# Graph attention and a transformer layer on one core: preparation steps in two halves, rows kept on chip, keys by transfer, tail loads and norms during attention

## The chip, the cores and the metric

The kernel runs on one core of a Trainium2 chip. The core has TensorE (matrix products, PE in the profile, with its weight loads as PEld), VectorE (DVE), ScalarE (ACT), GpSimd (POOL) and SyncE (SP), which here issues every transfer. The metric is the device time of one execution in microseconds (us), as a median of several runs.

## The reference

Two graph attention layers, then one transformer layer, over 4096 nodes with 256 features; `adj` is a 4096 x 4096 matrix of zeros and ones. Everything is float32.

```python
def gat_layer(x, adj, W, a):                  # 8 heads of 32
    Wh = einsum('nd,hdo->hno', x, W)
    src, dst = Wh . a[:, :32], Wh . a[:, 32:]
    e = leaky_relu(src[:, :, None] + dst[:, None, :], 0.2)
    alpha = softmax(where(adj > 0, e, -9e15))
    return heads_side_by_side(alpha @ Wh)

h = elu(gat_layer(x, adj, W1, a1)) + x
x = elu(gat_layer(h, adj, W2, a2)) + h

q, k, v = layer_norm(x, g1, be1) @ w_qkv      # 8 heads of 32
scores = where(adj != 0, q k^T / sqrt(32), -inf)
x = x + (softmax(scores) @ v) @ w_proj + b_proj
out = x + gelu(layer_norm(x, g2, be2) @ w1 + b1) @ w2 + b2
```

## The kernel before

The nodes are 32 tiles of 128. There are three stages, each in a function of its own or part of one.

**Graph attention** (`graph_attention`). The work of a layer is cut into groups: 4 blocks of 8 row tiles, times 4 pairs of heads, times 8 groups `g` of 4 column tiles, so 128 groups a layer and 256 in all, indexed by `i`. The exponential of a leaky ReLU factors on each side of its kink, so a group needs no exponential of its own: it needs a comparison of two terms per pair of nodes (`step` in `compare`, ScalarE's Sign at line 1100 or VectorE's comparison at line 1102), the adjacency laid over it as bits (line 1115, one VectorE operation a group) and then matmuls with the prepared values `vst` (line 1401, TensorE). Comparisons for group `i + 2` are made during group `i`.

Before a layer can run, `preparation(l, q, ...)` must make the values of eight groups of four tiles, `q` from 0 to 7. Its steps are: `features` (transposes at line 981 into a PSUM bank, ScalarE's copy at 984), `values` for each of four tiles (matmuls at 994 into a bank, then ScalarE's copy and three exponentials at 1001 to 1008, VectorE's maximum and product at 1009 and 1020), `split` (a float16 part and its remainder, 1032 to 1035, the last on GpSimd) and `term_rows` (one transpose, a copy and four small stores). For layer 0, `q` of 2 to 7 are prepared in groups 0 to 5; in the same groups the adjacency is read, clipped by VectorE (867) and turned by TensorE and ScalarE (`mask_turn`, 890 and 892). For layer 1, `q` of 0 to 5 are prepared in the last six groups of layer 0, and 6 and 7 in groups 131 and 132. Steps and turns take a bank from a ring of two (`turn_bank`).

Within a group all such extra steps are put into a list `side` with a place between 0 and 1, sorted by it, and emitted among the matmuls: after each of the group's eight row tiles come those whose place has been reached (lines 1401 to 1412). TensorE, ScalarE and VectorE run in exactly that order; SP and GpSimd are ordered by a scheduler outside the first lines. `pair_end` finishes a pair of heads in seven later steps; `step_out` adds the result to the layer's input and stores it, and `rows_ahead` loads four tiles of the stored rows for the preparation of the next layer.

**Query, key, value** (first part of `unshifted_transformer`). For each of 8 blocks of 512 nodes: norm, transposes, the projections (line 1677 for queries and keys, each stored to memory in a float16 part and its remainder; line 1696 for values). Keys are then loaded back by `stack` into `k_st`, which holds four stacked parts of 32 partitions for each head: two by transfer, the other two copied by VectorE at line 1710. Only SP's order is fixed here.

**Attention.** A unit is a block of queries, a half `c` of the heads (four, a quad) and one key tile, 512 units in all. A unit is scores (line 1734), the exponential (1741, ScalarE), the mask (1743, VectorE, two operations a unit), then the weighted sum of values (`u_av`, 1752) and the sum of weights (`u_dn`, also 1752); GpSimd adds the weights of two units first (`u_both`, 1825). At a quad's end the sums are stored, the denominators go to memory and back as `u_dens`, VectorE inverts them (1794) and the inverses are stored. TensorE, ScalarE and VectorE run in written order.

**The tail.** For each block of 512: load rows, attention sums and inverses (`rows_of`), apply bias and inverses, project (1888), add, norm (1448 to 1477), transpose (1490), first linear (1924) with GELU (1931), second linear (1940), store. The next block's projection stands ahead of the first linear. The scheduler orders all engines here.

Of the kernel before, what the change touches and what calls it, by code (L numbers as in the profile page):

```python
# [22 lines left out]
P = 128  # L23
# [728 lines left out]
def graph_attention(  # L752
# [127 lines left out]
    def mask_turn(nb, c, i):  # L880
# [8 lines left out]
        for m in range(G):  # L889
            nc.tensor.transpose(pt[:, m, :], v[:, m * P : (m + 1) * P], ident_h)  # L890
        to = built[nb, c][:, i // 2].bitcast(U16)
        nc.scalar.activation(to[:, :, i % 2 * P : (i % 2 + 1) * P], pt.bitcast(U16), AF.Copy)
        if i % 2 == 1:
            w = STARTS[0][nb] // PER + i // 2
            nc.sync.dma_start(
                mask_d[w][c], built[nb, c][:, i // 2].rearrange("p g n -> p (g n)").bitcast(U8)
            )

# [66 lines left out]
    def rows_ahead(l, q):  # L965
        if q < NG:
            coming_rows[l, q] = rows_p.tile([P, G, D], F32, name="g_rows")
            rows[l].load(coming_rows[l, q], G * q)

    def preparation(l, q, bank, first=False):  # L970
# [4 lines left out]
        def features(c):  # L975
# [3 lines left out]
            pt = bank()  # L979
# [4 lines left out]
            nc.scalar.copy(L.ft[q][:, c, :], pt)  # L984
            if c == DC - 1:
                del coming_rows[l, q]
                if (l > 0 or q > 1) and (l == 0 or q + 1 != NG - 2):
                    rows_ahead(l, q + 1)

        def values(t):  # L990
            at = G * q + t
            pv = bank()
            for c in range(DC):
# [7 lines left out]
            nc.scalar.copy(  # L1001
                L.terms[:, :, at, :], pv[:, D : D + 2 * H].rearrange("p (k h) -> p k h", k=2)
            )

            big = some.tile([P, 2, H], F32, name="g_big", bufs=4)
            for i, scale in enumerate((-1.0, -LRELU)):
                nc.scalar.activation(big[:, i, :], pv[:, D + H : D + 2 * H], AF.Exp, scale=scale)
            nc.scalar.activation(L.r[:, at, :], pv[:, D : D + H], AF.Exp, scale=LRELU - 1.0)
            nc.vector.tensor_reduce(
# [27 lines left out]
        def term_rows():  # L1037

            pr = bank()[: G * H, :P]
            nc.tensor.transpose(  # L1040
                pr, L.terms[:, 0, G * q : G * (q + 1)].rearrange("p t h -> p (t h)"), ident_f
            )
            sr = some.tile([G * H, P], F32, name="g_sr", bufs=1)
            nc.scalar.copy(sr, pr)
# [4 lines left out]
        steps = [lambda c=c: features(c) for c in range(DC)]  # L1049
        for t in range(G):  # L1050
            steps.append(lambda t=t: values(t))
            if t > 0:
                steps.append(lambda t=t: split(t - 1))
        return steps + [term_rows, lambda: split(G - 1)]
# [67 lines left out]
    def pair_end(l, nb, p, ev):  # L1122
# [6 lines left out]
        held = {}  # L1129
        wide = [P, n, 2, V1]  # L1130
# [51 lines left out]

        def step_out():
# [9 lines left out]
            [step_exp], [step_below, step_above], [step_out],  # L1193
# [55 lines left out]
    def begin():  # L1249
# [21 lines left out]
        first, second = (preparation(0, q, spare_bank, True) for q in range(2))  # L1271
        for step in first[:DC] + second[:DC]:
            step()
        for step in weights_steps(0):
            step()
        del first[:DC], second[:DC]
        value = [[steps[k] for k in (0, 1, 3, 5)] for steps in (first, second)]
        part = [[steps[k] for k in (2, 4, 6, 8)] for steps in (first, second)]
        row = [steps[7] for steps in (first, second)]
        for step in value[0][:2]:  # L1280
            step()
        for k in range(2):
            clip(k)
            value[0][2 + k]()
        row[0]()
        for k in range(4):
            value[1][k]()
            part[0][k]()
            if k < 2:
                clip(2 + k)  # L1290
            if k > 1:
                part[1][k - 2]()
        row[1]()
        s_of[0, 0, 0] = s_fetch(0, 0, 0)
        rows_ahead(0, 2)
        for k in range(4):
            turn(k)
            if k < 2:
                part[1][2 + k]()
# [16 lines left out]
    for i, (l, nb, p, g) in enumerate(groups):  # L1316
# [12 lines left out]
        if i + 1 in prepared and prepared[i + 1][0] > 0:  # L1329
            if prepared[i + 1][1] in (0, NG - 2):  # L1330
                rows_ahead(*prepared[i + 1])
        if made:
            steps = preparation(*made, lambda: turn_bank([P, 512], F32))
            if made[1] == NG - 1:
                steps.append(lambda: check_values(made[0]))
            beside(steps, 0.0, 0.9)
        if i + 2 < len(groups):
            steps = compare(i + 2)
            beside(steps[:-1], 0.25 if made else 0.0, 0.95)
# [8 lines left out]
        beside([lambda u=u: mask_turn(*u) for u in turns.get(i, ())], 0.0, 0.9)  # L1348
# [21 lines left out]
        for n in range(tiles):  # L1370
            w, at = n // PER, slice(n % PER * P, (n % PER + 1) * P)
            for m in range(G):
# [25 lines left out]
                for at_, (k, to, left, right) in enumerate(todo):  # L1398
# [3 lines left out]
                    opened.add(k)  # L1402
            if g == NG - 1:
# [7 lines left out]
            while side and (n == tiles - 1 or side[0][0] * tiles < n + 1):  # L1411
# [156 lines left out]
def unshifted_transformer(  # L1568
# [47 lines left out]
    dens = wts.tile([P, NQ, QI], F32, name="u_dens")  # L1616


    with ExitStack() as scope:
        vals = scope.enter_context(tc.tile_pool(name="u_vals", bufs=1))  # L1620
        k_st = vals.tile([P, DC * HC, N], F16, name="u_k")
        v_sb = vals.tile([P, NT, D], F32, name="u_v")
        blocks = scope.enter_context(tc.tile_pool(name="u_blocks", bufs=2))
        masks = scope.enter_context(tc.tile_pool(name="u_masks", bufs=5))
        block_tiles = {}

        def stack(to, i, order, cols):

            for a, kind in enumerate(order):
                if kind is None:  # L1630
                    continue
                first = half_d[i, kind, 0, 0:1, cols]
                nc.sync.dma_start(
                    to[a * O : (a + 1) * O],
                    spread(first, [[N, O], [O * N, DC * HC], [1, NB]]),
                )

        def load_queries(nb):
            q_st = blocks.tile([P, DC * HC, NB], F16, name="u_q")
            stack(q_st, 0, (0, 1, 0, 1), slice(nb * NB, (nb + 1) * NB))  # L1640
# [10 lines left out]
        with ExitStack() as qkv:  # L1651
# [8 lines left out]
            for nb in range(NNB):  # L1660
# [8 lines left out]
                if 2 < nb + 2 < NNB:  # L1669
                    ahead.moments(nb + 2)  # L1670
                    ahead.normed(nb + 2)
# [33 lines left out]
                for b in (nb - 1,) if nb + 1 < NNB else (nb - 1, nb):  # L1705
                    if b >= 0:
                        at = slice(b * NB, (b + 1) * NB)
                        stack(k_st[:, :, at], 1, (0, None, 1, None), at)
                        for o in (0, 2 * O):
                            nc.vector.tensor_copy(k_st[o + O : o + 2 * O, :, at], k_st[o : o + O, :, at])  # L1710
# [14 lines left out]
        def weights(nb, c, mt, u):  # L1725
# [4 lines left out]
            for j in range(2):  # L1730
                h = c * HC + 2 * u + j
                for r in range(HC):
# [3 lines left out]
                        k_st[:, h, at : at + O],  # L1736
# [64 lines left out]

# [261 lines left out]
```

## Time and profile before

| | us |
|---|---|
| three runs | 3217.39, 3220.55, 3221.06 |
| median | 3220.55 |
| profiled execution, device time | 3218.54 |
| its span in the profile | 3216.7 |
| PE busy in the span | 3091.4 (96%) |
| DVE busy | 2809.8 (87%) |
| ACT busy | 2667.1 (83%) |
| POOL busy | 1175.5 (37%) |

How to read it: a time in the page is one execution's. Graph attention lasts to about 1644 us, the query, key and value part to 1733, attention to 2926, the tail to the end. A busy share of 96% is an average over these; what is missing is in a few places, which a table of busy time by window shows. The chain of waits follows what ended last back to what released it, and so tells which wait counts.

### The profile page before, as it was taken

The numbers are of one execution on the slowest core, as the hardware profiler recorded it, in microseconds if no ns is written. First come the engines' busy times: TensorE is split into PE (matmuls) and PEld (weight loads), VectorE is DVE, ScalarE is ACT, GpSimd is POOL, SyncE is SP. The second block draws the span as 40 slices with busy tenths as digits, with TensorE's granted clock in tenths as the row PEclk, the third lists the DMA queues.
The fourth block names the chain that finished last, engine by engine and source line by source line (L and its number), as shares of the span: only waits on it lengthen the run. The fifth ranks groups of instructions, "written<-read, shape, count | busy, mean of one in ns | idle before, by whom it ended". The sixth has DMA issues, their size and how long they took to land.

```text
span 3216.7 us, 139103 instructions
## 1 busy us (share of the span) xinstructions
PE 3091.4 (96%) x64076; PEld 2713.3 (84%) x64076; DVE 2809.8 (87%) x3198; ACT 2667.1 (83%) x3175; POOL 1175.5 (37%) x536
## 2 busy tenths in 40 slices
PE   5899999999889999999998999999999999997999
PEld 4799999999779999999975888888888888885766
DVE  7899999989879999999986999999999999995221
ACT  6899999999779999999965888888888888884231
POOL 2300000000220000000002988899989889884110
PEclk8999999999999999999999999999999999998999
DMA  8666554420310312121145010101011010004110
GB/s 257 202 196 206 163 191 147 145 84 26 97 52 25 94 55 89 33 64 53 45 122 138 14 40 21 34 26 28 28 27 50 8 47 14 21 7 120 59 46 28
DMA packets 210305, 249.29 MB, mean 77 GB/s; under 512 B 87792, under 2 KB 131056, under 8 KB 209712
## 3 DMA queue, kind: packets, MB, share of 16 engines
q1 hardware_dynamic: 209712, 240.31, 24.5%
q8 instruction: 503, 8.24, 1.0%
q14 instruction: 90, 0.74, 0.1%
HBM read 197.80 MB, written 42.47 MB: 75 GB/s over the span
## 4 chain that ended last, share of the span: by engine, by line
PE 47%; DVE 3%; ACT 2%; DMA 1%; issue 0%; SPq 0%; DVEq 0%; ACTq 0%
PE u_ps L1734 15%; PE u_av L1752 14%; PE u_dn L1752 8%; PE misc L1940 3%; PE misc L1924 3%; PE misc L1677 2%; ACT t L1100 1%; DVE t L1115 1%; DVE t L1102 1%; PE misc L1696 1%; PE misc L1888 1%; PE misc L1490 0%; DVE u_e L1743 0%; DMA u_wide<-inv_d 0%; DVE u_k L1710 0%
## 5 line engine op out<-in xcount | busy, mean ns | idle before, releaser
L1401 PE MATMUL bank<-vst,t 128*128 128x132 f16 x16384 | 1449.8, 219 | 25.8 <-DVE t L1115 25.3
L1825 POOL TENSOR_TENSOR u_both<-u_e 128x1024 f32<-128x1024 f32 x448 | 1052.5, 2393 | 914.7 <-DMA u_k<-half_d 787.0
L1401 PE MATMUL bank<-vst,mask 128*128 128x66 f16 (+1 forms) x10296 | 1344.7, 206 | 0.0
L1100 ACT ACTIVATE t<-s_b,g_terms 128x1024 int8<-128x1024 f32 x1231 | 1318.5, 1155 | 27.4 <-PE bank L1401 21.6
L1401 PEld LDWEIGHTS <-t 128*128 128x128 fp8e4 x16384 | 1184.0, 97 | 40.2 <-DVE t L1115 29.7
L1743 DVE SCALAR_TENSOR_TENSOR u_e<-u_mask,u_ps 128x1024 f32<-128x1024 uint8 x1024 | 1165.9, 1214 | 9.2 <-ACT u_ps L1741 5.0
L1741 ACT ACTIVATE u_ps<-u_ps 128x1024 f32<-128x1024 f32 x1024 | 1030.0, 1009 | 141.8 <-PE u_ps L1734 45.6
L1401 PEld LDWEIGHTS <-mask 128*128 128x128 fp8e4 x10296 | 902.2, 98 | 0.0
L1115 DVE SCALAR_TENSOR_TENSOR t<-mask,t 128x2048 int32<-128x2048 int32 x256 | 591.0, 2309 | 73.6 <-ACT t L1100 63.1
L1734 PE MATMUL u_ps<-u_q,u_k 128*32 128x512 f16 x8192 | 636.6, 383 | 10.4 <-DVE u_e L1743 7.8
L1752 PE MATMUL u_av<-u_e,u_v 128*32 128x128 f32 x16384 | 601.2, 273 | 0.0
L1752 PEld LDWEIGHTS u_av<-u_e,u_v 128*32 128x32 f32 x16384 | 487.6, 110 | 130.1 <-issue 1.7
L1102 DVE TENSOR_SCALAR t<-s_b,g_terms 128x1024 fp8e4<-128x1024 f32 x817 | 583.8, 747 | 2.6 <-DMA s_b<-s_d 2.6
L1035 POOL TENSOR_TENSOR vst<-g_prod,vst 128x528 f16<-128x528 f32 x36 | 44.0, 1236 | 778.0 <-DVE vst L1034 757.7
L1752 PE MATMUL u_dn<-u_both,u_ones 128*32 128x128 f32 x7168 | 279.6, 273 | 0.0
L1734 PEld LDWEIGHTS <-u_k 128*32 128x32 f16 x8192 | 227.4, 95 | 57.9 <-issue 16.4
L1752 PEld LDWEIGHTS u_dn<-u_both,u_ones 128*32 128x32 f32 x7168 | 212.2, 110 | 41.4 <-issue 0.4
L1931 ACT ACTIVATE u_hid<-misc,n_b 128x512 f32<-128x512 f32 x64 | 42.4, 687 | 152.5 <-PE misc L1924 152.4
L1947 DVE TENSOR_TENSOR u_xres<-u_xres,misc 128x256 f32<-128x256 f32 x32 | 13.5, 421 | 141.9 <-PE misc L1940 141.9
L1940 PE MATMUL misc<-u_w,u_hid 128*128 128x256 f32 x512 | 111.8, 379 | 0.0
L1924 PE MATMUL misc<-ln_cols,u_w 128*128 128x512 f32 x256 | 111.2, 592 | 0.0
L1940 PEld LDWEIGHTS misc<-u_w,u_hid 128*128 128x128 f32 x512 | 96.7, 190 | 13.3 <-issue 0.5
(145 smaller groups left out, 1865.3 us busy)
## 6 DMA issues: line engine op xcount, KB each, us to landing
g_adj<-in_adj_dram SPq DMA_DIRECT2D x123, 512.0 KB
s_b<-s_d SPq DMA_DIRECT2D x64, 512.0 KB
mask<-mask SPq DMA_DIRECT2D x128, 256.0 KB
u_mask<-mask SPq DMA_DIRECT2D x32, 512.0 KB
mask<-stage SPq DMA_DIRECT2D x48, 256.0 KB
rows<-e_x SPq DMA_DIRECT2D x32, 256.0 KB
half_d<-u_halves SPq DMA_DIRECT2D x32, 256.0 KB
u_q<-half_d SPq DMA_DIRECT2D x32, 256.0 KB
```

Of the source, the lines that this page charges most:

```text
L1100: nc.scalar.activation(to.bitcast(I8), s, AF.Sign, bias=negd, scale=-1.0)
L1102: nc.vector.tensor_scalar(to, s, negd, -1.0, op0=ALU.is_ge, op1=ALU.mult, saturate=False)
L1115: nc.vector.scalar_tensor_tensor(both, m32.unsqueeze(1).to_broadcast(list(both.shape)), SIGNS, both, op0=ALU.bitwise_or, op1=ALU.bitwise_and,)
L1401: nc.tensor.matmul(to, left, right, start=k not in opened, stop=last)
L1677: nc.tensor.matmul(pq, wq_sb[k][:, i * D + c * P : i * D + (c + 1) * P], hn[:, k, :], start=(k == 0), stop=(k == DC - 1),)
L1734: nc.tensor.matmul(ps[r * O : (r + 1) * O, j, :], k_st[:, h, at : at + O], q_st[:, h, :], start=True, stop=True,)
L1741: nc.scalar.activation(ps, ps, AF.Exp, scale=SCALE)
L1743: nc.vector.scalar_tensor_tensor(e, mask, 0.0, ps, op0=ALU.not_equal, op1=ALU.mult)
L1752: nc.tensor.matmul(to[j * O : (j + 1) * O, at], lefts[j], es[j // 2][:, j % 2, at], start=first and part == 0, stop=last and part == PARTS ...
L1825: nc.gpsimd.tensor_tensor(both, es_of[i - 1][u], es_of[i][u], op=ALU.add)
L1924: nc.tensor.matmul(ph, w1_sb[:, k, f * P : (f + 1) * P], hn[:, k, :], start=(k == 0), stop=(k == DC - 1),)
L1940: nc.tensor.matmul(po[:, :D], hid[:, f, at : at + P], w2_sb[:, f, :], start=(f == 0), stop=(f == FC - 1),)
```

## The change

It has five parts.

1. *Steps in two halves.* In `preparation`, each use of a bank is split into an `_out` half (TensorE) and an `_in` half (ScalarE and VectorE); `mask_turn` likewise. A group places the two halves and `split` by slots, turns and values taking turns in layer 0. Side steps are emitted after each of a group's 32 sets of matmuls and no longer after each of its 8 row tiles. In `values`, the exponentials come ahead of the copy.

```diff
+    def features_out(c):
+        pt = held["f", c] = bank()
+        for t in range(G):
+            nc.tensor.transpose(...)
+    def features_in(c):
+        nc.scalar.copy(L.ft[q][:, c, :], held.pop(("f", c)))
...
+            uses = list(features)
+            delay = 0.3 if turning else 0.6
+            for t in range(G):
+                if turning:
+                    u = turning.pop(0)
+                    uses.append((lambda u=u: turn_out(*u), lambda u=u: turn_in(*u)))
+                uses.append(values[t])
+            uses.append(term_rows)
+            slot = 0.9 / len(uses)
+            for k, use in enumerate(uses):
+                side.append(((k + 0.5) * slot, use[0]))
+                side.append(((k + 0.5 + delay) * slot, use[1]))
+                if use in values:
+                    side.append(((k + 2.0 + delay) * slot, splits[values.index(use)]))
...
-            beside(steps[:-1], 0.25 if made else 0.0, 0.95)
+            beside(steps[:-1], 0.3 if made else 0.0, 0.95)
...
+                while side and side[0][0] * tiles * G < n * G + m + 1 and not (
+                    n == tiles - 1 and m == G - 1
+                ):
+                    side.pop(0)[1]()
...
-            while side and (n == tiles - 1 or side[0][0] * tiles < n + 1):
+            while side and n == tiles - 1:
```

2. *Rows kept.* The last pair of layer 0's last block writes its result straight into the row tiles that `q` of 6 and 7 of layer 1 read; their other columns are loaded at the layer's start.

```diff
+        keeps = l + 1 < NL and first + n == NT and p + 1 == H // 2
...
+        def step_out_and_keep():
+            x, ex = held["x"], held["ex"]
+            for k in range(n // G):
+                to = coming_rows[l + 1, first // G + k][:, :, cols]
+                nc.vector.tensor_tensor(to..., x[:, k * G : (k + 1) * G], ex[...], op=ALU.add)
+                nc.sync.dma_start(rows[l + 1].blocks[nb][...], to)
...
+        if l > 0 and (nb, p, g) == (0, 0, 0):
+            for q in (NG - 2, NG - 1):
+                rows_ahead(l, q, D - 2 * O)
```

3. *Keys.* `k_st` is two tiles, one for each half of the heads. For the last three blocks all four parts come by transfer. A one-element exponential after the last norm brings ScalarE's table in early.

```diff
+                        for c in range(DC):
+                            late = b >= NNB - 3
+                            kinds = (0, 0, 1, 1) if late else (0, None, 1, None)
+                            stack(k_st[c][:, :, at], 1, kinds, at, c, HC)
+                            for o in () if late else (0, 2 * O):
+                                nc.vector.tensor_copy(
+                                    k_st[c][o + O : o + 2 * O, :, at], k_st[c][o : o + O, :, at]
+                                )
...
+                        nc.scalar.activation(rooted, ahead.held[nb + 2][:, 0, 1:2], AF.Exp)
```

4. *Loads and first operations during attention.* At the fifth unit of the last quad, `load_early` loads the tail's weights and biases and the rows, sums and inverses of blocks 0 and 1, into the key tile of the first half of the heads, and into a query and a mask buffer. GpSimd applies bias and inverses. A one-element root follows the last exponential.

```diff
+                    if u == 0 and units[i] == (NNB - 1, DC - 1, 4):
+                        load_early()
...
+            for k, unit in enumerate(((NNB - 1, DC - 1, NT // 2 - 1), units[-1])):
+                if i < len(units) and units[i] == unit:
+                    res, att, inv = early[k]
+                    nc.gpsimd.tensor_tensor(
+                        res, res, early["bp"].to_broadcast([P, TB, D]), op=ALU.add
+                    )
+                    nc.gpsimd.tensor_tensor(att, att, inv, op=ALU.mult)
+            if i == len(units) - 1:
+                nc.scalar.activation(rooted, norms.eps, AF.Sqrt)
...
+            slab = slab_p.tile([P, 32 * D], F32, name="u_k0")
+            two = blocks.tile([P, 2, TB * D], F32, name="u_q")
+            for nb in range(2):
+                load_rows(nb, *early[nb])
```

5. *Order of the tail.* Blocks 0 and 1 are projected first; block `nb + 2` is projected after the first linear of block `nb`. TensorE runs in written order. The check of the denominators comes at block 2.

```diff
+        scope.enter_context(tc.manual_schedule(engines={mybir.EngineType.PE}))
+        ready = [projected(*early[nb][:2]) for nb in range(2)]
+        coming = rows_of(2)
+        hn = turned(ready[0][1])
...
         for nb in range(NNB):
+            res, res_n = ready.pop(0)
...
-                res_next, res_n = projected(*rows_of(nb + 1))
...
+            if nb + 2 < NNB:
+                ready.append(projected(*coming))
+                if nb + 3 < NNB:
+                    coming = rows_of(nb + 3)
             if more:
-                hn = turned(res_n)
+                hn = turned(ready[0][1])
```

## The prediction

> **What bounds the kernel now.** I read the 40 slices first, then busy time by window, then the chain of waits and the VectorE timeline inside the windows that were not full.
>
> The slices (PE = TensorE, DVE = VectorE; each digit is a tenth of a slice of 80.4 us):
>
> ```profile
> PE   5899999999889999999998999999999999997999
> DVE  7899999989879999999986999999999999995221
> PEclk8999999999999999999999999999999999998999
> ```
>
> TensorE is full nearly everywhere. There are four dents: the first two or three slices, slices 11 and 12, slice 22, and slice 37. Busy time in windows cut at those dents (start:end, length, then busy us of PE, weight load, DVE, ACT, POOL, then granted clock, DMA share, GB/s):
>
> ```profile
> 91.80:107.90 16.10, 12.39 (x149) 10.48 (x149) 11.81 (x23) 11.08 (x31) 9.13 (x6) 1.00 0.67 216
> 834.10:847.40 13.30, 10.80 (x133) 9.30 (x131) 12.04 (x22) 8.08 (x26) 5.12 (x5) 1.00 0.21 60
> 922.20:941.30 19.10, 15.33 (x157) 13.55 (x157) 9.63 (x19) 9.29 (x28) 4.26 (x4) 0.82 0.24 69
> 1733.00:1760.00 27.00, 16.87 (x272) 10.88 (x276) 25.41 (x20) 15.03 (x17) 13.90 (x5) 0.75 0.53 118
> 1790.00:2926.50 1136.50, 1134.90 (x32664) 916.24 (x32652) 1123.63 (x1002) 1004.36 (x1018) 1013.47 (x433) 1.00 0.10 26
> 2926.50:2961.60 35.10, 14.54 (x40) 11.46 (x41) 12.04 (x32) 2.42 (x4) 6.97 (x3) 0.61 0.68 200
> 2961.60:3209.00 247.40, 247.40 (x921) 169.76 (x919) 49.77 (x148) 70.50 (x98) 30.55 (x13) 1.00 0.16 50
> ```
>
> Attention (fifth line) and the feed-forward (last) have no idle TensorE to win. What can be won lies in the others: groups that also prepare values (first three), the start of attention, and the gap before the feed-forward. The timeline of line 1115 (one mask operation per group) gives their lengths: the six groups that prepare for layer 0 start 14.05, 15.40, 14.45, 16.11, 15.39 and 14.87 us apart (90.3), the first six for layer 1 take 83.4 us, and its last two 19.0 and 15.1. A group without preparation takes about 5.2 to 6.3.
>
> The start of attention, chain of waits (start, length, what):
>
> ```profile
> 1737.61 3.48 DVE u_e L1743 x3
> 1741.12 1.22 DVE u_k L1710
> 1742.37 2.35 DVE u_e L1743 x2
> 1744.75 3.20 DVE u_k L1710
> ```
>
> VectorE's key copies (L1710) stand in the queue between the score masks (L1743) that TensorE waits for. The gap before the feed-forward, same view:
>
> ```profile
> 2926.83 3.10 DMA den_d<-u_den
> 2930.01 4.04 DMA u_dens<-den_d
> 2943.75 9.86 DMA u_wide<-inv_d
> 2953.72 1.24 DVE u_att L1884
> 2955.01 6.78 PE misc L1888 x16
> 2961.79 13.73 PE misc L1924 x32
> ```
>
> Here the end waits for transfers: the last denominators go out and back, then loads for block 1 stand behind two weight loads of 1 MB.
>
> **What the skill says.** "TensorE: Matmul & The Clock Gate", "What's actually happening": the array starts throttled, and only sustained work releases it. The trace agrees: granted clock 0.61 in the gap, 0.75 at the start of attention, 1.00 in full windows. So a gap costs more than its idle time. "DMA: Bandwidth & Descriptors", "Queues, rings and completion order": each engine takes descriptors in ring order, and all of SP's transfers share one row. The trace agrees: a 128 KB load took 9.86 us behind the weights. This is my warning for loads moved into attention. "ScalarE: Activation LUTs", "What ACT_TABLE_LOAD costs", gives about 1283 ns plus a drain; the trace has 1283 ns.
>
> **The change, part by part** (against the profiled execution: 3218.54 us, span 3216.7).
>
> *Loads and norms ahead (the end).* Weights, biases and rows, attention and inverses of blocks 0 and 1 are loaded in the last quad (a block's four heads), and POOL applies bias and inverses there. After the last attention matmul (about 2925.2) TensorE can project at once, with full clock. Two projections (L1888 x16, 3.45 us each for later blocks in the chain) end at 2932.1. Block 0's chain on VectorE: the last add comes about 3.6 us after the start; behind it stand 2 adds and 2 statistics of block 1's (0.42 each) and an aggregate or two (0.18), then the inverse (0.17) and four norms (1.38): about 7.6 us. Transposes of the last tile and ScalarE's ln_cols (0.78 each, two, partly overlapped) make some 9. The first L1924 then starts at 2934.3, where it now starts at 2961.6: 27.3 us gained. Both cases have the same work behind that point, 247.4 us of full TensorE; moving a projection from before the first linear to behind it changes no total. The last denominators still travel, but only block 7's projection needs them. Bounds: 24 (VectorE's order delays the norm) to 28. The Sqrt table is loaded after the last exponential, beside matmuls: nothing.
>
> *What that costs in attention.* SP can issue the early loads once the last read of the first key half is done, about 2846 (3 us before VectorE's first mask of the last quad). Some 2 MB go before the quad's denominators, w1 (1 MB) just before, w2 just behind them. Now u_dens is issued at 2858.9 and VectorE's reciprocal stands at 2864.6, with the masks (1.146 us each: 73.35 us a quad over 64) queued behind it. At 200 to 300 GB/s (windows above, slices) w1 delays the denominators by 1 to 2 us and w2 the reload by 3 to 5, so the reciprocal is late by about 1, 0 to 4. If the whole 4 MB stood ahead it would be 20 us; that end is a rival. POOL gets four operations of 2.35 us; TensorE reads u_both some 4.5 us after it is ready (u_both ends 2856.4, read 2861.0). Two fall into the quad's idle POOL time of 3.7 us, but one of them waits for its load, and one follows the first pair: about 5.1 us late against 4.5, cost about 1, 0 to 4. Together I take 2, range 0 to 8.
>
> *Keys by transfer.* The six copies of the last three blocks on VectorE between 1735.03 and 1754.9 (2.47 for two, then 1.22, 3.20, 1.22, 2.02) go; the earlier blocks' are only cut in halves. Thirteen masks are done at 1761.6 now; from 1737.61 at 1.146 each they would be at 1752.5: 9.1 gained, plus about 0.4 since the Exp table is loaded earlier (the load stands at 1735.08, first exponential 1736.37), less some slow clock. I take 9.3, bounds 6 (slow clock lasts) and 11. In exchange SP issues 24 transfers instead of 6, about 0.5 us each: 9 us more, and 1.5 MB more. Those keys are first used 20 units of 2.29 us into attention, 46 us later, so that hides; SP's following query load is wanted two quads later.
>
> *Split bank steps.* Nothing is removed. TensorE's half and the reading half get separate places, at a step of 1 in 32 of a group instead of 1 in 8, and ScalarE may do comparisons between them. A preparing group has 11 to 12.4 us of TensorE and 10.4 to 13.1 of VectorE against 13.3 to 16.1, so the most that could go is about 2.5 a group. But two banks serve all steps: a value step holds one for TensorE (1.0 us), three exponentials (0.2 each), a reduction and a product (0.42, 0.68), some 2.7 plus what stands ahead on ScalarE and VectorE, four times a group, and in layer 0 turns and values alternate, so that values always get the same bank. I take 0.85 a group for these twelve: 10. Bounds: minus 3 to 28, since no row shows the new order.
>
> *Rows kept.* Layer 1's last two groups (19.0 and 15.1) no longer wait for the row's way to memory and back (longest wait there 3.4 us, then a clock of 0.82). TensorE's 15.33 busy at 0.82 are 12.5 at full clock. I take 13 for each: 8.5, bounds 3.4 and 11. VectorE pays two adds of half size (0.42) for one of 0.69.
>
> Sum: 27.3 + 9.3 + 10 + 8.5 - 2 = 53.1; 3218.5 - 53.1 = 3165.4. The median shown is 2.0 above the profiled execution, so 3167.4.
>
> **Rivals** (medians).
> - The split gains nothing, the banks bind as now: only 3.4 of the rows is left. 27.3 + 9.3 + 3.4 - 2 = 38: 3182.5. For it: VectorE is 12.04 of 13.30 busy already. Against: in the window from 91.80 no engine is busy for more than 12.4 of 16.1 us.
> - The split brings preparing groups near the busiest engine, 12.6 in layer 0 and 11.6 in layer 1: 14.7 + 13.8, rows 10. With the rest 73.1: 3147.5.
> - The early loads delay the denominators of the last quad by the whole 4 MB, VectorE's reciprocal holds the masks for 20 us: 3187. For it: ring order, as above. Against: most of it is issued 11 us before.
> - Slower: value steps sharing one bank stretch each of the 14 preparing groups, since the read half now comes later behind comparisons. It decides from 3.2 us a group (the 38 of the first rival and 6.4, over 14). At 4 us a group: 3220.5 - 38 + 56 = 3238.5. Against: the reading half is moved by a third to six tenths of a slot only, under 0.5 us of matmuls.
>
> **How the numbers follow.** Forecast 0.62, no gain from the split 0.18, near the floor 0.10, loads in the way 0.05, slower 0.05. The range 3149 to 3187 holds the forecast with its bounds, the first rival and half of the second. A difference under 0.2% (6.4 us) can't be told from none here; all cases but the last are faster by more, so faster 0.94, same 0.01, slower 0.05.
>
> **What would show it.** Right: the first L1924 (now another line) within 10 us of the last attention matmul, at a clock near 1; no key copy among the first masks, and the first 13 of these in about 15 us; preparing groups of 14 and 13 us; no group of 19. Wrong: an idle VectorE ahead of u_inv in the last quad; TensorE waiting for u_both there; a VectorE or ScalarE queue that keeps the turn banks, with preparing groups as long as now.

## The result and the profile after

The changed kernel takes 3169.9 us (median of 4 runs, 3168.24 to 3172.45), the kernel before 3218.97 in its runs beside it: ratio 0.985, 95% interval 0.983 to 0.987. The forecast was 3167.4. The profiled execution has a span of 3168.0 us, 48.7 less than before. The slices after:

```profile
PE   6999999999989999999999999999999999999999
DVE  7899999989899999999985999999999999998221
PEclk8999999999999999999999999999999999999999
```

The dents of TensorE at slices 11, 22 and 37 are gone, one at slice 12 and the ones at the start remain. Busy time in windows cut at the mask operation (one a group, now line 1129): the six preparing groups of layer 0, the first six of layer 1, and layer 1's last two with the groups around them.

```profile
48.40:132.40 84.00, 70.78 (x862) 60.75 (x860) 73.92 (x132) 64.80 (x172) 34.86 (x23) 1.00 0.74 228
815.00:890.40 75.40, 66.30 (x812) 57.96 (x810) 66.87 (x118) 54.16 (x162) 36.40 (x22) 1.00 0.40 118
890.40:954.60 64.20, 56.60 (x966) 53.59 (x963) 60.71 (x84) 52.44 (x91) 17.77 (x10) 1.00 0.12 35
```

Before, the same stretches took 90.3, 83.4 and 69.0 us:

```profile
47.93:138.20 90.27, 74.16 (x903) 62.88 (x901) 73.60 (x137) 64.24 (x177) 35.43 (x24) 0.99 0.66 211
820.62:903.98 83.36, 72.33 (x859) 62.67 (x858) 66.98 (x118) 55.01 (x161) 28.52 (x24) 0.96 0.33 103
```

VectorE and ScalarE have the same work in them within 0.9 us, and VectorE now is busy for 88 and 89% of the first two. TensorE's records show 41 and 47 matmuls fewer in them. A stretch is cut at VectorE's mask operations, and part of TensorE's work now falls into the group behind it: the group behind the first stretch takes 8.0 us instead of 6.7, the one behind the second 9.7 instead of 8.1. So of the 6.3 and 8.0 us by which the first two are shorter, some is only moved: with the next two groups counted in, the first gains 5.7; with the next three, the second gains 6.0. The start of attention, VectorE's timeline (start, length, what, and idle time before it):

```profile
1720.09 15.93 DVE L1818 SCALAR_TENSOR_TENSOR u_e<-u_mask,u_ps 128x1024 f32<-128x1024 uint8 x14 [2.71 <-ACT u_ps L1816]
1737.60 8.01 DVE L1818 SCALAR_TENSOR_TENSOR u_e<-u_mask,u_ps 128x1024 f32<-128x1024 uint8 x7 [1.58 <-ACT u_ps L1816]
```

Fourteen masks stand back to back with no copy between them; then comes a pause of 1.58 us. Before, pauses of 0.83 and 0.16 us stood about there. The last quad, idle time of TensorE, and then the chain of waits at its end:

```profile
2832.56 0.86 PE L1827 MATMUL u_av<-u_e,u_v 128*32 128x128 f32 x24 [1.32 <-issue]
2837.40 0.64 PE L1827 MATMUL u_av<-u_e,u_v 128*32 128x128 f32 x16 [0.29 <-issue]
2843.37 0.30 PE L1827 MATMUL u_dn<-u_both,u_ones 128*32 128x128 f32 x2 [0.77 <-POOL u_both L1936]
```

```profile
2902.95 0.48 PE u_dn L1827 x16
...
2903.49 0.59 ACT u_den L1860
2904.09 0.04 issue
2904.13 7.17 PE misc L1985 x32
2911.30 0.50 PE misc L1545 x4
...
2911.89 0.79 ACT ln_cols L1548
2912.68 0.04 issue
2912.72 14.00 PE misc L2024 x32
```

No transfer is left in this chain. From the last attention matmul to the first linear it takes 9.3 us, before 36.4. From there to the end it is 255.3 us (before 255.1).

### The profile page after: what moved, and what is told of

Same layout as the page of the kernel before. It is cut to its first block, busy times and chain, and to the rows that moved or that the text cites. A ratio compares the mean times of both kernels' runs of the same rounds, so it can differ in the third digit from the quotient of the medians.

```text
span 3168.0 us, 139144 instructions
## 1 busy us (share of the span) xinstructions
PE 3073.6 (97%) x64076; PEld 2705.3 (85%) x64076; DVE 2809.0 (89%) x3201; ACT 2668.9 (84%) x3177; POOL 1197.6 (38%) x538
## 3 DMA queue, kind: packets, MB, share of 16 engines
q8 instruction: 503, 8.24, 1.1%
## 5 line engine op out<-in xcount | busy, mean ns | idle before, releaser
L1114 ACT ACTIVATE t<-s_b,g_terms 128x1024 int8<-128x1024 f32 x1231 | 1318.9, 1157 | 31.4 <-PE bank L1452 24.4
L1818 DVE SCALAR_TENSOR_TENSOR u_e<-u_mask,u_ps 128x1024 f32<-128x1024 uint8 x1024 | 1166.1, 1215 | 15.1 <-ACT u_ps L1816 10.2
L1049 POOL TENSOR_TENSOR vst<-g_prod,vst 128x528 f16<-128x528 f32 x36 | 59.5, 1669 | 748.2 <-DVE vst L1048 735.6
L2044 PE MATMUL misc<-u_k,u_hid 128*128 128x256 f32 x512 | 111.8, 379 | 0.0
L2024 PE MATMUL misc<-ln_cols,u_k 128*128 128x512 f32 x256 | 111.3, 593 | 0.5 <-ACT ln_cols L1548 0.5
L2044 PEld LDWEIGHTS misc<-u_k,u_hid 128*128 128x128 f32 x512 | 96.7, 190 | 13.3 <-issue 0.5
L2024 PEld LDWEIGHTS misc<-ln_cols,u_k 128*128 128x128 f32 x256 | 48.6, 190 | 58.5 <-issue 56.9
```

The costliest lines, as they stand in the source:

```text
L1049: nc.gpsimd.tensor_tensor(halves[:, :, 1, :], part, halves[:, :, 0, :], op=ALU.subtract)
L1114: nc.scalar.activation(to.bitcast(I8), s, AF.Sign, bias=negd, scale=-1.0)
L1818: nc.vector.scalar_tensor_tensor(e, mask, 0.0, ps, op0=ALU.not_equal, op1=ALU.mult)
L2024: nc.tensor.matmul(ph, w1_sb[:, k, f * P : (f + 1) * P], hn[:, k, :], start=(k == 0), stop=(k == DC - 1),)
L2044: nc.tensor.matmul(po[:, :D], hid[:, f, at : at + P], w2_sb[:, f, :], start=(f == 0), stop=(f == FC - 1),)
```

## The experiments

Every kernel below was timed with runs of the kernel before beside it (their median was 3217.4 for the first four, 3219.3 for the next four, 3217.6 for the last). Since effects of 2 to 5 us are near what the total can tell, I read them from stages of the trace. The table holds, in us: the median; layer 0's six preparing groups; layer 1's first six; the stretch of its last two; from the first attention mask to the first denominators' reciprocal; from the fourteenth reciprocal to the last attention matmul; from there to the first linear.

| kernel | median | L0 | L1 | last two | start | last quads | to linear |
|---|---|---|---|---|---|---|---|
| before | 3219.0 | 90.3 | 83.4 | 69.0 | 97.8 | 134.0 | 36.4 |
| changed | 3169.9 | 83.9 | 75.4 | 64.2 | 90.1 | 137.3 | 9.3 |
| steps_whole | 3181.7 | 90.6 | 83.5 | 62.8 | 88.6 | 138.3 | 9.3 |
| halves_together | 3181.5 | 80.8 | 84.7 | 69.7 | 90.2 | 137.3 | 9.3 |
| halves_coarse | 3175.1 | 84.7 | 75.4 | 67.7 | 91.4 | 137.3 | 9.3 |
| rows_back | 3177.5 | 83.9 | 75.4 | 69.6 | 90.5 | 138.3 | 9.3 |
| keys_copied | 3182.2 | 83.9 | 75.4 | 65.4 | 99.4 | 138.3 | 9.3 |
| layer0_together | 3167.0 | 82.0 | 75.4 | 65.4 | 90.0 | 137.8 | 9.3 |
| steps_whole_fine | 3177.8 | 90.3 | 81.7 | 62.4 | 90.4 | 138.3 | 9.3 |
| paced | 3180.6 | 83.9 | 75.4 | 65.4 | 90.1 | 143.3 | 9.3 |
| slab_after | 3178.5 | 84.8 | 75.4 | 65.4 | 90.1 | 134.0 | 20.9 |
| burst_and_order | 3182.4 | 83.9 | 75.4 | 66.8 | 89.5 | 138.6 | 23.3 |
| turns_after | 3175.3 | 89.5 | 75.4 | 65.4 | 90.0 | 136.9 | 9.3 |
| act_paced | 3166.1 | 82.0 | 75.4 | 65.4 | 88.7 | 137.5 | 9.3 |

A stage before attention that a kernel does not touch repeats within 1 us, the last two groups' stretch within 2.6. In attention the same code differs by some us: see the last section.

**Preparation put back whole.**

```diff
-                side.append(((k + 0.5) * slot, use[0]))
-                side.append(((k + 0.5 + delay) * slot, use[1]))
...
+            def whole(use):
+                return lambda: (use[0](), use[1]())
+            beside(steps, 0.0, 0.9)
...
+            while side and (n == tiles - 1 or side[0][0] * tiles < n + 1):
```

> The preparation steps of graph attention are put back as before: both halves of a bank use at one place, the old order of steps, places only after each row tile, statistics from 0.25. Everything else as changed. Theory A (these places and halves made the preparing groups shorter): the six preparing groups of layer 0 go back from 84.0 to about 90 us and the first six of layer 1 from 75.4 to about 83, so the whole is 12 to 16 us slower (about 3182 to 3186). Theory B (the twelve groups got shorter through something else, such as rows already in SBUF or the order of the exponentials): these sums stay within 3 us of 84.0 and 75.4, the whole under 5 us slower.

90.6 and 83.5, 14.8 us more together, and 11.8 in the median: theory A holds. The part of the new steps is real and larger than I forecast. The third stretch is 1.4 us shorter than in the changed kernel: the group behind layer 1's six and the one behind its last two are 1.7 and 2.1 us shorter, while group 6 (the first of the last two) takes 12.8 us instead of 10.4. With the groups behind counted in, the new steps are worth 12.6 us.

**Halves apart or together, fine places or coarse.** In halves_together the reading half has no delay; in halves_coarse the emission between a tile's matmuls is taken out.

```diff
-                side.append(((k + 0.5 + delay) * slot, use[1]))
+                side.append(((k + 0.5) * slot, use[1]))
```

> As changed, but the reading half of each bank use comes at the same place as TensorE's half; slots, order and the fine places stay. Theory A1 (it is the distance between the halves that helps): layer 0 and layer 1 groups lose most of the 14.3 us, the whole is 8 to 14 us slower. Theory A2 (it is the fine places and the turns between values that help): the two sums rise by less than 4 us together.

> As changed, halves apart, but steps are only given out after a row tile (8 places a group), no longer between its matmuls (32 places). Theory A1 (the distance between halves helps): a slot of 0.9/9 of a group is about a tile, so the halves still lie a tile apart and the sums stay within 4 us. Theory A2 (fine places help): the whole is 8 to 14 us slower, sums near 90 and 83.

Neither theory holds for both layers. With the halves together layer 1 loses 9.3 us in its six groups and 5.5 in its last two, as A1 says, but layer 0 gains 3.1: the delay harms it. Coarse places cost 0.7 in layer 0 and nothing in layer 1's six; 3.4 in the last two. So in layer 1 the gain needs the distance. The waits in layer 1's six groups (us in total, times, longest), with halves together:

```profile
DVE g_prod L1034 <- POOL vst L1049: 19.8, 14, 2.8
PE turn L1054 <- DVE g_prod L1034: 14.6, 6, 2.5
ACT g_sr L1060 <- PE turn L1054: 14.4, 6, 2.6
```

and in the changed kernel:

```profile
DVE g_prod L1034 <- POOL vst L1049: 6.2, 6, 1.4
PE turn L1054 <- DVE g_prod L1034: 4.6, 5, 1.3
ACT g_sr L1060 <- PE turn L1054: 0.7, 1, 0.7
```

The transpose of the term row (L1054) needs a bank that VectorE's product (L1034) still holds, and the product itself waits for GpSimd's remainder (L1049). With both halves at one place ScalarE's reading half (g_sr) sits in its queue meanwhile, 2.4 us a group, with all comparisons behind it. Put later, it waits 0.7 us in all.

The old order of steps did not have this wait. In steps_whole, same six groups:

```profile
ACT g_big L1018 <- PE turn L1005: 17.8, 17, 3.1
ACT g_sr L1060 <- PE turn L1054: 0.7, 2, 0.4
```

There ScalarE waits for the values' matmuls instead, 17.8 us against 10.6 in the changed kernel. So the distance keeps the new order from bringing a wait of its own; what in the new order removed the old wait of layer 1 was not taken apart.

**Layer 0.** Three kernels take it apart. steps_whole_fine gives the old list out at fine places; layer0_together keeps the halves together in layer 0 only; turns_after is that kernel with the mask turns at places of their own. With the turns out of the list, its values stand 0.13 of a group apart and no longer 0.16, and two of its four turns still fall between values.

```diff
+                side.append(((k + 0.5 + (delay if made[0] else 0.0)) * slot, use[1]))
...
-                if turning:
+                if False:
                     u = turning.pop(0)
```

> As changed, but with the old list of steps (whole steps, turns after the values, statistics from 0.25) given out at the new fine places between a tile's matmuls. Theory A5 (layer 0 gains from turns between values and parts two slots later, not from fine places): layer 0's six groups stay near 90, layer 1's near 83, the whole 11 to 15 us slower. Theory A2 (fine places): layer 0 falls to 84 or below.

> As changed, but in layer 0, where mask turns alternate with values, the reading half of a bank use comes at the same place as TensorE's half; layer 1 keeps the distance. Theory A3 (between two banks that alternate turn and value, a later read only keeps the bank longer; in layer 1 it fills TensorE's wait): layer 0's six groups fall from 84.0 to about 81, layer 1's six stay at 75.4 within 0.5, the whole 2 to 4 us faster than the changed kernel. Theory A4 (the two stages depend on each other through the statistics ahead): layer 1 changes by more than 2 us.

> As the kernel with layer 0's halves together, but the mask turns of layer 0 are spread over the group at places of their own instead of one ahead of each value step. Theory A5 (a turn ahead of each value gives every value step the same bank with a turn's time to come free, which is what layer 0 gained): its six groups go back from 82.0 to 88 or more, the whole 6 to 9 us slower than that kernel. Rival A6 (new slots, parts two slots later and the statistics' later start are what gained): under 84.

The fine places alone give layer 0 nothing (90.3) and layer 1 1.8 us. Layer 0 falls to 82.0 with halves together while layer 1 stays at 75.4 (A3), and goes back to 89.5 when the turns have places of their own (A5's number). So its gain is the list in which a turn comes one place ahead of each value; how much of that is the turn and how much the wider spacing of the values was not taken apart. What TensorE and ScalarE wait for in layer 0's six groups, in turns_after:

```profile
ACT g_big L1018 <- PE turn L1005: 20.7, 20, 3.2
PE turn L1005 <- DVE ev_broad L1040: 6.3, 5, 2.0
```

in layer0_together:

```profile
ACT g_big L1018 <- PE turn L1005: 7.4, 17, 0.9
PE turn L1005 <- ACT mask L898: 5.2, 18, 0.6
```

and in the changed kernel:

```profile
ACT g_big L1018 <- PE turn L1005: 16.1, 22, 1.3
PE turn L1005 <- ACT t L1114: 7.0, 12, 1.5
PE turn L1005 <- DVE ev_broad L1040: 3.3, 4, 1.1
```

The largest difference is ScalarE's: the value's reading half (g_big) stands in its queue until TensorE has made the value (L1005), 20.7 us in turns_after and 7.4 in layer0_together. TensorE in turn waits for a bank. In turns_after that is up to 2.0 us for another value's product (ev_broad; L1034 is the operation that reads the bank, L1040 the one behind it). In layer0_together all 18 waits end 0.05 us after the copy of the turn just ahead (L898), 14 of them before the product of the value before has ended: a value takes over the turn's bank, and waits 0.6 at most.

With the halves apart it is the other way. In the changed kernel 15 of the 24 values begin 0.15 us after the product (L1034) of the value before has ended, most of them while the turn between is still being copied: values keep to one bank and wait for each other, mostly 0.5 to 0.7 us. The profile puts 11 of these 15 waits down to a comparison (t, L1114) that ended at about the same time; but in the other four the distance to the product is the same, so I take it for the product. Values that share one bank were the mechanism of my slower rival. It exists, at 2 to 3 us for six groups instead of 24.

**Rows through memory again.**

```diff
-        keeps = l + 1 < NL and first + n == NT and p + 1 == H // 2
+        keeps = False
...
-        if l > 0 and (nb, p, g) == (0, 0, 0):
-            for q in (NG - 2, NG - 1):
-                rows_ahead(l, q, D - 2 * O)
```

> As changed, but layer 1's last two row groups again go through memory and back in whole (VectorE adds in one operation and nothing is kept). Theory R1 (the row's wait is what was gained, and part was given back by the groups after): group 6 goes back from 10.4 to about 19 us, the stretch from the first of the last two to the last group's end from 64.2 to about 68 to 69, the whole 4 to 5 us slower. Theory R2 (my prediction's 8.5): 8 to 9 us slower. Theory R3: the split steps would have hidden the wait anyway, under 2 us slower.

The median is 7.6 us slower, but only 5.4 of it are in the stage: group 6 takes 15.8 us, not 10.4, and not the 19.0 of before, so the split steps had already taken 3.2 of its wait. TensorE waits 2.2 us there for the row. R1's size holds for the stretch (4.2 to 5.4, since its other groups repeat only within 1.2), R1's 19 us does not. The groups behind the six and behind the last two take 9.7 and 7.2 us as in the changed kernel, where steps_whole has 8.1 and 5.0 as before; so what these two lost belongs to the split, not to the rows. The rest of the median is not the rows': in the profile, attention, whose code is the same, is 3.4 us longer, with 8.2 us of stalls marked issue against 3.9.

**Keys copied again.**

```diff
-                            late = b >= NNB - 3
+                            late = False
```

> As changed, but the keys of the last three blocks are again copied by VectorE instead of coming by transfer. Theory K1 (my prediction's 9.3, of which the changed kernel showed 7.4 because the added 1.5 MB leave TensorE without instructions for 1.7 us): VectorE's copies stand between the first masks again, the stretch from the first mask to the first reciprocal goes from 90.1 back to about 97.8, the stall of TensorE marked issue among the first masks (1.67 us at 1735.60) is gone or under 0.3 us, the whole 7 to 8 us slower. Theory K2 (the stall has nothing to do with transfers): the stall stays at 1.5 us or more and the stretch is about 99.5.

Of the twelve half-size copies four stand just ahead of the first mask and eight between the first masks, where before four whole ones stood. The first of these eight (VectorE's timeline):

```profile
1720.55 2.35 DVE L1818 SCALAR_TENSOR_TENSOR u_e<-u_mask,u_ps 128x1024 f32<-128x1024 uint8 x2
1722.94 0.68 DVE L1783 COPY u_k<-u_k 32x2048 f16<-32x2048 f16 x1
1723.65 1.22 DVE L1818 SCALAR_TENSOR_TENSOR u_e<-u_mask,u_ps 128x1024 f32<-128x1024 uint8 x1
1724.90 3.43 DVE L1783 COPY u_k<-u_k 32x2048 f16<-32x2048 f16 x2
```

Both theories are half right. No stall among the first masks is marked issue any more, as K1 says, but TensorE waits for masks there in the meantime (3.25 us at the longest), and a stall could hide in these waits. The stretch is 99.4, as K2 says, 9.4 more than in the changed kernel: the copies in halves cost more than the whole ones did (97.8).

**Early loads spaced by SP's written order.** Attention runs SP in written order; block 1 and the pieces of w1 and w2 are written one in every second unit.

```diff
+        ordered.add(mybir.EngineType.SP)
...
+                    if u == 0 and paced and units[i][2] > 7 and i % 2 == 0:
+                        paced.pop(0)()
```

> As changed, but SP's work in attention follows the written order, and of the early loads only the projection's weight, the biases and block 0 come at once; block 1 and eight pieces of w1 and w2 (256 KB each) follow one in every second unit. Theory F (a burst of transfers delays TensorE's own instruction loads): the stalls marked issue in the last quad (1.6 us) fall under 0.4 us, the last 14 to 16 units' masks no longer wait, the stretch from the fourteenth reciprocal to the last attention matmul falls from 137.3 to about 134, the whole 2 to 4 us faster. Theory P (POOL's four added operations cost it): the stretch stays above 136.

A miss, and a useful one: it is 11 us slower. The loads wait for nothing, so SP issued them all between 2838 and 2860, where their places in the program are spread over 22 units (some 50 us): an order is not a clock. And now the 2 MB written ahead of the reload of the denominators (u_dens) stand ahead of it: SP issues it 7.5 us after the store it follows, in all other quads but the last 2.1 to 2.4. VectorE's timeline:

```profile
2850.90 0.25 DVE L1869 RECIPROCAL u_inv<-u_dens 128x16 f32<-128x16 f32 x1 [6.13 <-DMA u_dens<-den_d]
```

The masks behind the reciprocal wait 6.1 us. This is my rival of loads that hold the denominators, met here and not in the changed kernel. The Trainium skill, "DMA: Bandwidth & Descriptors", "Queues, rings and completion order", has descriptors taken in ring order on each DMA engine. Here some 5 of the 6.1 us lie in the later issue by SP; what the rings add, no run here separates.

That is half of the loss. The other 5 us lie before the last quads. SP's written order now puts each block's query load and a mask load next to each other, and TensorE stalls behind them in six blocks, 0.7 to 1.8 us each and 7.6 in all (0.6 in the changed kernel), the first of them here:

```profile
1892.57 0.52 PE L1827 MATMUL u_av<-u_e,u_v 128*32 128x128 f32 x10 [1.07 <-issue]
```

**The slab over the other half of the keys.**

```diff
-            pool.tile([P, HC, N], F16, name=f"u_k{c}") for c, pool in enumerate((slab_p, vals))
+            pool.tile([P, HC, N], F16, name=f"u_k{c}") for c, pool in enumerate((vals, slab_p))
...
-            slab = slab_p.tile([P, 32 * D], F32, name="u_k0")
+            slab = slab_p.tile([P, 32 * D], F32, name="u_k1")
```

> As changed, but the slab of early loads lies over the second half of the keys, which attention reads to its end: projection weight, biases, block 0's rows, attention and inverses, w1 and w2 can only start with the last scores; block 1's loads stay early. Theory T (my prediction: the end was gained by loads that no longer stand behind attention, at a small cost in the last quad): from the last attention matmul to the first linear it takes 20 to 28 us instead of 9.3, and the last quad is free of w1, w2 and POOL's bias operations, so the stretch from the fourteenth reciprocal to the last attention matmul falls from 137.3 to about 134; the whole 8 to 15 us slower. Rival T2 (the end was gained by the order of projections): the gap stays under 14 us.

Both numbers of theory T came: 20.9 and 134.0. TensorE sits idle 10 us at the end:

```profile
2910.65 4.64 PE L1985 MATMUL misc<-u_k 128*128 128x256 f32 x10 [10.03 <-POOL u_k L1953]
```

So the early loads of the slab, with GpSimd's operations on them, are worth 11.6 us at the end and cost 3.3 in the last two quads.

**A burst, and the order of projections.** One kernel, two stages.

```diff
+            if (nb, k) == (4, 1):
+                for copy in range(8):
+                    nc.sync.dma_start(burst_d[copy], b.rearrange("p m n -> p (m n)"))
...
-            if nb + 2 < NNB:
-                ready.append(projected(*coming))
             hid = tail.tile([P, FC, NB], F32, name="u_hid")
```

(The projection's lines come ahead of `hid`.)

> As changed, with two edits far apart. In attention on block 3, after a mask chunk for block 4 has landed, eight copies of it (512 KB each, 4 MB) go out to memory, which nothing waits for. And in the feed-forward the projection of block nb + 2 comes before block nb's first linear instead of behind it. Theory F (dense transfers keep TensorE without instructions): within 25 us of the eight copies TensorE stalls for 1 to 2.5 us marked issue, at a place where no other program has a stall. Rival F2 (the stalls near query loads are something else): no stall there above 0.3 us. Order of projections: block 2's product of attention and inverse is ready 16 us after attention's end in the changed kernel, so the gap to the first linear grows from 9.3 to about 17; if it stays near 11 (two projections and transposes only), the order gained nothing.

The eight copies were issued from 2259.1 to 2267.4. TensorE's timeline:

```profile
2267.77 0.49 PE L1831 MATMUL u_av<-u_e,u_v 128*32 128x128 f32 x9 [0.30 <-issue]
2273.16 0.49 PE L1831 MATMUL u_av<-u_e,u_v 128*32 128x128 f32 x9 [0.84 <-issue]
...
2924.92 6.76 PE L1989 MATMUL misc<-u_k,u_att 128*128 128x256 f32 x16 [7.80 <-DVE u_att L1981]
```

No other program here has a stall at this place, so dense transfers do cause them, though 1.1 us in two pieces is the low end of F, and this is one trace. The last line is the other edit: the projection of block 2 waits 7.8 us for its loads, then runs at about half speed (6.76 us at a granted clock of 0.54; 3.62 at 1.00 in the changed kernel). The gap grows by 13.9 us, more than I expected; 3.6 of that is work which only moved.

**Early loads issued by ScalarE.** On layer0_together: rows, sums and inverses of blocks 0 and 1, w1 and w2, one or two issues a unit.

```diff
+                    if u == 0 and units[i][:2] == (NNB - 1, DC - 1) and units[i][2] in paced:
+                        paced.pop(units[i][2])()
```

> As the kernel with layer 0's halves together, but the early loads of blocks 0 and 1, w1 and w2 are issued by ScalarE, one to three a unit, from the sixth to the twenty-third unit of the last quad, so that its own order spaces them; SP keeps only the projection's weight and the biases. ScalarE pays 18 issues of about 0.4 us. Theory F (a dense burst is what stalls TensorE): stalls marked issue from the fourteenth reciprocal on fall under 0.5 us and the stretch to the last attention matmul from about 138 to 134 to 135.5; the whole 2 to 4 us faster, about 3164. Rival (each piece stalls TensorE, or ScalarE's issues hold the exponentials): the stretch stays at 137 or more.

In the last quad no stall marked issue is left, so spaced pieces do not starve TensorE; but the stretch is 137.5, as the rival says. What stands there now (TensorE's and then VectorE's waits in the last quad):

```profile
PE u_dn L1827 <- POOL u_both L1966: 1.9, 1, 1.9
DVE u_e L1818 <- POOL u_both L1966: 2.3, 2, 1.2
```

VectorE's waits point to POOL's added operations: 2.3 us for its sums against 0.6 for exponentials. How much of the 3.5 us over slab_after is POOL's and how much ScalarE's issues (0.4 us each, sixteen) is open. With 3166.1 (ratio to before 0.984, interval 0.982 to 0.986) it is the shortest median. It can't be told from layer0_together's 3167.0 (0.984, 0.983 to 0.986), nor that from the changed kernel by totals alone; the 2.0 us of layer 0 repeat in both.

## Why the prediction was right, and where it was not

- **The end, 27.3.** 27.1. The projection, norm and transposes follow at full clock as worked out. (The items of VectorE's chain add up to 7.0 to 7.2 us, where I wrote 7.6; from the first projection to the last norm the trace has 7.3.) slab_after shows that 11.6 of it are the slab's loads; burst_and_order that 13.9 would be lost if block 2's projection stood ahead. "Moving a projection changes no total" was right for the work, but the move also hides block 2's loads; the sum was right since it counted only two projections.
- **Its cost in attention, 2.** 3.3 by the last two quads, and slab_after shows that it goes away when the slab's loads and GpSimd's operations on them come after attention. The mechanism was half wrong: the denominators were not late, as VectorE has no idle time before u_inv. Instead TensorE stalled for 1.6 us while w1 and w2 came in, a cost that I had put on no transfer; the waiting for POOL's sums (0.8) was as forecast.
- **Keys, 9.3.** The first thirteen masks took 14.8 us instead of 24.0, 9.2 where the sum had 9.1. The 0.4 for the earlier table did not come: the first mask stands 2.5 us after the first scores, before 2.4. Then VectorE paused 1.58 us because TensorE stood for 1.67, so the first reciprocal came 7.8 nearer to the first mask. In act_paced that stall was 0.48 and the stretch 88.7, in steps_whole 0.27 and 88.6. The term was right, and the stall was missing from the sum. (The mark alone does not find it: in layer0_together TensorE stands 1.87 us at the same place, put down to a mask that had ended 0.9 us before, and the stretch is 90.0.)
- **Split steps, 10 (bounds -3 to 28).** 14.3 by the two stretches, 12.6 by steps_whole with the groups behind counted in: the size was off, since no row showed the new order. One cause that I named is there, the distance between the halves, which layer 1 needs. The other I had the wrong way round. I named turns and values alternating as what holds the gain back, because the values would always get the same bank. In the runs a turn ahead of each value is what layer 0 gains by (89.5 to 82.0), and values keep to one bank only when the halves are apart, which costs 2 to 3 us. So this term came near its number in part by luck.
- **Rows kept, 8.5.** Two groups of 13 against 19.0 and 15.1 make 8.1, not 8.5. Group 6 did as I took it: with the rows kept and whole steps (steps_whole) it takes 12.8, and the split brings it to 10.4. The failed step was group 7. I gave it the same 13 from group 6's busy time, and read no line of its own. Before:

```profile
941.28:956.40 15.12, 14.29 (x205) 12.99 (x205) 13.92 (x27) 11.40 (x29) 5.52 (x5) 1.00 0.01 3
```

TensorE was busy for 14.29 of its 15.12 us at a clock of 1.00, so the row's wait held nothing back there, and it still takes 15.3. The rows alone gave 6.2 (steps_whole against before), and 5.4 where the split had taken part of the wait (rows_back).

The sum of parts, 18.5 for the split and the rows, came to 19.0 in the three stretches and to 17.5 by the first mask of attention (1737.61 to 1720.09); where the 1.5 between went was not traced. The terms' errors cancelled in part, which is luck: some 2.6 too little for the split, 2.3 too much for the rows, 1.5 too much for the keys, 1.3 too little cost.

## What to carry to other kernels

Where a few banks serve many users, ask of each who holds the bank and who stands queued behind the reader: here a short user ahead of each long one, or the reading half moved behind other work of its engine, removed waits, and the same delay did harm in a stage with another pattern. Loads moved under busy engines are not free even when nobody waits for their data: price the burst itself, and space it by a real dependence or another engine's order, for a written order of issues spaces nothing. Where parts of some us are to be compared, read the stage in the trace, since the total moves by as much from stalls elsewhere.

## What the runs showed of the hardware

TensorE's stalls marked issue stand beside dense transfers. In the changed kernel's last quad, the window with w1 and w2 (busy us of the engines, clock, DMA share, GB/s) and one that begins 8 us after it:

```profile
2829.00:2836.00 7.00, 5.68 (x172) 4.45 (x167) 5.61 (x5) 5.46 (x7) 6.72 (x3) 1.00 0.99 306
2844.00:2850.00 6.00, 6.00 (x172) 5.12 (x168) 5.93 (x6) 5.04 (x5) 6.00 (x3) 1.00 0.01 3
```

In other programs whose attention is written the same the stall in the last quad was 2.2 (rows_back) and 2.5 us (steps_whole), and in mid-attention those that I placed stand within about 12 us of a block's query load, or the mask load behind it, or block 1's early loads; they add up to 0.6 us in the changed kernel and 2.9 in keys_copied. The profile lists a queue for instructions:

```profile
q8 instruction: 503, 8.24, 1.1%
```

8.24 MB in 503 packets are 16 KB each. That TensorE then waits for such a packet behind data fits all of this, and is argued, not shown; that transfers cause the stalls is shown by the burst and by the six blocks of paced, and that spacing them removes them by act_paced, each in one trace.
